# A graph network's layer on one core: projections of x on four 64x64 tiles of the array, with half of x brought across the partitions by DMA, and the second layer's weights prepared earlier

## The chip, the cores and the metric

The kernel runs on one core of a Trainium2 chip. Its time is the device time of one execution in microseconds (us), the median of several executions. The profile is of one such execution; its span, from the first to the last instruction, is somewhat shorter than the time.

## The reference

There are 16 batches of 1024 nodes with 64 channels, and one adjacency matrix of 1024 x 1024. Layer 0 is attention whose weights are multiplied by the adjacency matrix; layer 1 is a diffusion convolution. Each adds its input and normalises. Cut to what matters:

```python
# layer 0: x is (16, 1024, 64), adj (1024, 1024)
Q = einsum('bnc,oc->bno', x, Wq) + bq
K = einsum('bnc,oc->bno', x, Wk) + bk
V = einsum('bnc,oc->bno', x, Wv)
score = softmax(einsum('bnc,bmc->bnm', Q, K), axis=1)   # over the queries n
score = einsum('bnm,mc->bnc', score, adj)
x = layernorm(x + einsum('bnm,bmc->bnc', score, V))
# layer 1: x0 = x, x1 = adj x0, x2 = 2 adj x1 - x0, for two supports that are both adj
x_cat = concatenate([x0, x1, x2, x1, x2], axis=-1)
out = layernorm(x + einsum('bnf,fo->bno', x_cat, weight) + bias)
```

## The kernel before

All is fp32. The batches are worked on in eight pairs (p), so that two times 64 channels fill the 128 partitions. The kernel does three things one after another:

- It forms U = adj x for all batches, a product of 1024 x 1024 x 1024, by seven products of half the size instead of eight (numbered 1 to 7; 2, 3 and 4 are each split again into seven parts). TensorE multiplies, VectorE forms the sums of blocks and adds the results. The left and right sums need room, and they borrow GY, which is not needed yet.
- It runs the attention, pair by pair, in eight steps of 128 nodes (m). The scores are x M x with M = Wq Wk, so that one projection GY = M x + a bias per pair does for both Q and K. A step forms scores on TensorE, VectorE copies them out negated with their least value (e), ScalarE takes the exponentials, TensorE multiplies them with U scaled (us) and sums over the steps (acc). Scores and exponentials run two steps ahead of the multiplication.
- It multiplies adj twice more for layer 1 and normalises.

The projection uses a matrix of 128 x 128 with M in two diagonal blocks and zeros elsewhere (m_w). The code below holds the parts that the change and the prediction touch; xT of a pair is made by eight transposes on TensorE and a copy on ScalarE, and `centre` subtracts the mean of x on GpSimd.

```python
# xT[:, p]: pair p of batches, channels on the partitions (2 x 64), nodes along the row
# GY[:, p]: the projected x of pair p, in the same layout
    def transposed(p, pt=None):

        pt = ps_tile("pt") if pt is None else pt
        for k in range(K8):
            nc.tensor.transpose(pt[:, ts(k, P)], xs[:, p, k, :], ident)
        nc.scalar.activation(xT[:, p], pt, AF.Copy)
    # ...
    def score_weight(pw):
        nc.tensor.transpose(pw[:, 0:P], wq, ident)
        nc.tensor.transpose(pw[:, P : 2 * P], wk, ident)
        nc.vector.tensor_copy(wn, pw[:, 0 : 2 * P].rearrange("p (a o) -> p a o", a=2))

    def score_weight_2(pm):
        nc.tensor.matmul(pm[:, 0:P], wn[:, 1], wn[:, 0], start=True, stop=True)
        nc.tensor.matmul(pm[:, H : H + 1], wn[:, 0], bkp, start=True, stop=True)
        nc.vector.tensor_copy(m_w, pm[:, 0:P])
        nc.vector.tensor_copy(gb, pm[:, H : H + 1])
    # ...
    def project(p, pg=None):
        pg = ps_tile("pg") if pg is None else pg
        for h in range(2):
            nc.tensor.matmul(pg[:, ts(h, H)], m_w, xT[:, p, ts(h, H)], start=True, stop=True)
        nc.scalar.activation(GY[:, p], pg, AF.Identity, bias=gb, scale=1.0)
    # ...
    def layer_weights():
        w24 = const.tile([P, C], FP, tag="w24", name="w24")
        nc.vector.tensor_add(w24, w1s[:, 2], w1s[:, 4])
        nc.vector.tensor_sub(raw[:, 0], w1s[:, 0], w24)
        nc.vector.tensor_add(raw[:, 0], raw[:, 0], ident[:, 0:C])
        nc.vector.tensor_add(raw[:, 0], raw[:, 0], ident[:, C:P])
        nc.vector.tensor_add(raw[:, 1], w1s[:, 1], w1s[:, 3])
        nc.vector.tensor_scalar(raw[:, 2], w24, 2.0, None, op0=ALU.mult)
        rsum = const.tile([P, 5], FP, tag="rsum", name="rsum")
        nc.vector.tensor_reduce(rsum, raw, AX.X, ALU.add)
        nc.vector.scalar_tensor_tensor(
            raw, rsum[:, :, None].to_broadcast([P, 5, C]), -1.0 / C, raw, op0=ALU.mult, op1=ALU.add
        )
        wv = pair_weight("wv")
        for j in range(2):
            s = slice(j * C, (j + 1) * C)
            nc.vector.tensor_copy(wv[s, s], raw[s, 3])
        return wv
    # ... each product of left and right sums is four matmuls deep; step() is its matmuls, some
    # queued VectorE pieces (fill) and the eviction (read); part() is one of seven sub-products
        def step(self, name, g, fills=0, rows=(0, 1)):
            self.matmuls(name, g, rows)
            fill(fills)
            self.read(name, g, rows)
    # ...
    def scores(n):

        p, m = steps[n]
        sc = [ps_tile(f"sc{j}") for j in range(2)]
        for h in range(2):
            for j in range(2):
                s = slice(j * C, (j + 1) * C)
                nc.tensor.matmul(
                    sc[j][:, ts(h, H)], GY[s, p, ts(m, P)], xT[s, p, ts(h, H)],
                    start=True, stop=True,
                )
        NM[n] = small.tile([P, 2], FP, tag="nm", name="nm")
        E[n] = att.tile([P, 2, N], FP, tag="e", name="e", bufs=3)
        for j in range(2):
            nc.vector.tensor_scalar(
                E[n][:, j], sc[j], -1.0, None, op0=ALU.mult, op1=ALU.min,
                accum_out=NM[n][:, j : j + 1],
            )
        SM[n] = small.tile([P, 2], FP, tag="es", name="es")
    # ...
    def weighted(n):
        p, m = steps[n]
        if m == 0:
            ACC[p] = pacc.tile([P, N], FP, tag="acc", name="acc")
        es, us = E.pop(n), US.pop(n)
        for h in range(2):
            for j in range(2):
                nc.tensor.matmul(
                    ACC[p][j * C : (j + 1) * C, ts(h, H)], us[:, j], es[:, j, ts(h, H)],
                    start=(m == 0), stop=(m == K8 - 1),
                )
    # ...
    def centre(p):
        nc.gpsimd.tensor_tensor(
            rows_of(p), rows_of(p), mu[:, p, :, None].to_broadcast([P, G, C]), ALU.subtract
        )
```

The order of work from product 2 to the first steps of the attention (h[0] to h[3] are PSUM tiles; later() queues VectorE pieces, fill and need issue them):

```python
    for q in PARTS:                       # (1, 2, 6, 5, 7, 3, 4)
        first.part(2, q, two, {1: 0, 3: 2, 4: 2}.get(q, 1))
    need("T1", "S1")
    first.step(5, 0, 8)
    # ... product 5's other half, product 3
    score_weight(h[3])
    transposed(0, h[2])
    need("T2")
    lefts, rights = first.halves(4, room[1])
    later("half", lefts)
    later("mu", [
        lambda p=p: nc.vector.tensor_reduce(mu[:, p], rows_of(p), AX.X, ALU.add)
        for p in range(NP)
    ])
    first.step(6, 0, 5)
    score_weight_2(h[3])
    transposed(1, h[2])
    first.step(6, 1, 6)
    project(0, h[3])
    transposed(2, h[2])
    need("S3", "T3")
    line[:0] = [("T4", f) for f in first.right_sum(4)]
    first.step(7, 0, 6)
    project(1, h[3])
    transposed(3, h[2])
    line[:0] = [("half", f) for f in rights]
    first.step(7, 1, 6)
    project(2, h[2])
    project(3, h[3])
    need("T4", "half")
    for q in PARTS:
        first.part(4, q, two)
        if q == 6:
            scores(0)
            for j in range(2):
                exponentials(0, j)
    need("mu")
    nc.vector.tensor_scalar(mu, mu, 1.0 / C, None, op0=ALU.mult)
    nc.sync.dma_start(aT[:, low, right], a_in[:, low, right])
    scores(1)
    for j in range(2):
        exponentials(1, j)
    transposed(4)
    scaled(0)
    wv = layer_weights()
    for p in range(5):
        centre(p)
```

The loop over the steps:

```python
    for n, (p, m) in enumerate(steps):
        if (p, m) == (NP - 2, 2):
            later("half", both(*hop_1.halves(2, room[0])))
        if n + 2 <= last:
            scores(n + 2)
            exponentials(n + 2, 0)
        if p and m > 4:
            weigh(p - 1, m - 5)
        elif p > 1 and m == 0:
            weigh(p - 2, 3)
        elif p == 0 and m:
            if m % 2:
                project(m // 2 + 4)
            else:
                transposed(m // 2 + 4)
                centre(m // 2 + 4)
        if n + 1 <= last:
            scaled(n + 1)
        if m <= 4:
            fill(1)
        weighted(n)
        if m == K8 - 1:
            take(p)
        if n + 2 <= last:
            exponentials(n + 2, 1)
        if p:
            if m == 0:
                norm_1(p - 1)
            elif m == 1:
                norm_2(p - 1)
            elif m == 4:
                transposed(p - 1)
```

Of the kernel before, what the change touches and what calls it, by code (L numbers as in the profile page):

```python
# [9 lines left out]
FP = mybir.dt.float32  # L10
# [8 lines left out]
def gnn_kernel(  # L19
# [13 lines left out]
    nc = tc.nc  # L33
    ctx.enter_context(tc.manual_schedule())
    N, B, C = out.shape
    P = 128
# [3 lines left out]
    H = 512  # L40
# [4 lines left out]
    const = ctx.enter_context(tc.tile_pool(name="const", bufs=1))  # L45
# [5 lines left out]
    def ps_tile(name):  # L51
        return ps.tile([P, 2 * H], FP, tag="ps", name=name)
# [7 lines left out]
    def pair_weight(name):  # L60
        w = const.tile([P, P], FP, tag=name, name=name)
        nc.vector.memset(w, 0.0)
        return w
# [37 lines left out]
    xT = big.tile([P, NP, N], FP, tag="xT", name="xT")  # L101
    GY = big.tile([P, NP, N], FP, tag="gy", name="GY")
    mu = const.tile([P, NP, G], FP, tag="mu", name="mu")
    wn = const.tile([P, 2, P], FP, tag="wn", name="wn")
    m_w = const.tile([P, P], FP, tag="m_w", name="m_w")
    gb = const.tile([P, 1], FP, tag="gb", name="gb")

    def transposed(p, pt=None):

        pt = ps_tile("pt") if pt is None else pt  # L110
        for k in range(K8):
            nc.tensor.transpose(pt[:, ts(k, P)], xs[:, p, k, :], ident)  # L112
        nc.scalar.activation(xT[:, p], pt, AF.Copy)

    def score_weight(pw):
        nc.tensor.transpose(pw[:, 0:P], wq, ident)
        nc.tensor.transpose(pw[:, P : 2 * P], wk, ident)
        nc.vector.tensor_copy(wn, pw[:, 0 : 2 * P].rearrange("p (a o) -> p a o", a=2))

    def score_weight_2(pm):  # L120
        nc.tensor.matmul(pm[:, 0:P], wn[:, 1], wn[:, 0], start=True, stop=True)
        nc.tensor.matmul(pm[:, H : H + 1], wn[:, 0], bkp, start=True, stop=True)
        nc.vector.tensor_copy(m_w, pm[:, 0:P])
        nc.vector.tensor_copy(gb, pm[:, H : H + 1])

    def rows_of(p):
        return xs[:, p].rearrange("p k (b c) -> p (k b) c", b=2)

    def project(p, pg=None):
        pg = ps_tile("pg") if pg is None else pg  # L130
        for h in range(2):
            nc.tensor.matmul(pg[:, ts(h, H)], m_w, xT[:, p, ts(h, H)], start=True, stop=True)  # L132
        nc.scalar.activation(GY[:, p], pg, AF.Identity, bias=gb, scale=1.0)

    def idle_turns(n):
# [12 lines left out]
# [18 lines that stand above are left out]
# [52 lines left out]
    def by_pair(t):  # L218

        return t.rearrange("p k (q f) -> p q k f", f=P)  # L220
# [4 lines left out]
    def later(name, pieces):  # L225
        line.extend((name, piece) for piece in pieces)

    def fill(n):
        for _ in range(min(n, len(line))):
            line.pop(0)[1]()  # L230

    def need(*names):
        while any(name in names for name, _ in line):
            fill(1)
# [159 lines left out]
# [20 lines that stand above are left out]
    def exponentials(n, j):  # L414
        nc.scalar.activation(  # L415
            E[n][:, j], E[n][:, j], AF.Exp, bias=NM[n][:, j : j + 1], scale=-1.0,
            accum_out=SM[n][:, j : j + 1],
        )

    def scaled(n):  # L420

        p, m = steps[n]
        ri = small.tile([P, 2], FP, tag="ri", name="ri")
        nc.vector.reciprocal(ri, SM.pop(n))
        US[n] = small.tile([P, 2, C], FP, tag="us", name="us")
        nc.vector.tensor_tensor(  # L426
            US[n], U[:, m, ts(p, P)].rearrange("p (b c) -> p b c", b=2),
            ri[:, :, None].to_broadcast([P, 2, C]), ALU.mult,
# [13 lines that stand above are left out]
# [7 lines left out]
# [4 lines that stand above are left out]
# [44 lines left out]
    def both(lefts, rights):  # L497
        return [f for pieces in zip(lefts, rights) for f in pieces]

    S = left_tiles()  # L500
    h = [ps_tile("h0"), ps_tile("h1"), pacc.tile([P, N], FP, tag="acc", name="h2"), ps_tile("h3")]
    two = h[2:]
    first = Product(S, xs, by_pair(U), h, None, (2, 3, 4))
# [7 lines left out]
    for n in (1, 2, 4):  # L511
        later(f"S{n}", left_sum(S, n))
    for q in PARTS:
        first.part(2, q, two, {1: 0, 3: 2, 4: 2}.get(q, 1))
    need("T1", "S1")
    first.step(5, 0, 8)
    need("S4")
# [6 lines left out]
    for q in PARTS:  # L524
        first.part(3, q, two)
    score_weight(h[3])
    transposed(0, h[2])
    need("T2")
    lefts, rights = first.halves(4, room[1])
    later("half", lefts)  # L530
# [2 lines left out]
        for p in range(NP)  # L533
    ])
    first.step(6, 0, 5)
    score_weight_2(h[3])
    transposed(1, h[2])
    first.step(6, 1, 6)
    project(0, h[3])
    transposed(2, h[2])  # L540
    need("S3", "T3")
    line[:0] = [("T4", f) for f in first.right_sum(4)]
    first.step(7, 0, 6)
    project(1, h[3])
    transposed(3, h[2])
    line[:0] = [("half", f) for f in rights]
    first.step(7, 1, 6)
    project(2, h[2])
    project(3, h[3])
    need("T4", "half")  # L550
# [10 lines left out]
    for j in range(2):  # L561
        exponentials(1, j)
    transposed(4)
    scaled(0)
    wv = layer_weights()
    for p in range(5):
        centre(p)

# [7 lines left out]
# [8 lines that stand above are left out]
        elif p > 1 and m == 0:  # L584
            weigh(p - 2, 3)
        elif p == 0 and m:
            if m % 2:
                project(m // 2 + 4)
            else:
                transposed(m // 2 + 4)  # L590
                centre(m // 2 + 4)
        if n + 1 <= last:
            scaled(n + 1)
        if m <= 4:
# [13 lines that stand above are left out]
    p = NP - 1  # L608
# [6 lines left out]
    h = [pacc.tile([P, N], FP, tag="acc", name="h0")] + [ps_tile(f"h{n}") for n in (1, 2, 3)]  # L615
# [8 lines left out]
    two = (h[2], h[3])  # L624
# [18 lines left out]
    two = (h[1], h[3])  # L643
# [136 lines left out]
```

## Time and profile before

| what | value |
|---|---|
| time, median of 3 | 621.12 us (620.71 to 621.95) |
| span of the profiled execution | 619.2 us |
| mean granted TensorE clock | 0.986 |
| U = adj x and what is done beside it | to about 113 us |
| attention | about 104 to 417 us |
| layer 1 | from about 417 us on |

The profile's groups that the change touches (line, engine, output<-input, instructions, busy us, mean ns of one): an fp32 matmul shows as two instructions, so the projections of eight pairs are 32 of them.

| group | instructions | mean or median |
|---|---|---|
| L132 PE, projections beside the products (h) | 16 | 592 ns |
| L132 PE, projections in the attention (pg) | 16 | 592 ns, the longest 1220 |
| L133 ACT, their eviction to GY (pg) | 4 | 1094 ns |
| L401 PE, scores, two 64x128 tiles of the array | 512 | 621 ns |
| L438 PE, acc, two 128x64 tiles of the array | 512 | 605 ns |
| L408 DVE, copy of the scores with their least value | 128 | 1222 ns |
| L415 ACT, exponentials | 128 | 1143 ns |

In the profile PE is TensorE's matmuls, PEld its weight loads, DVE VectorE, ACT ScalarE, POOL GpSimd. A busy row gives the time in which an engine had an instruction at work. Matmuls overlap in the pipeline, so their lengths do not add up; the chain of waits gives each piece's share of the path instead. A matmul that stands on two tiles of the array at once shows as two rows of about the same start. An arrow in brackets behind a row of the timeline names the engine and line that ended the idle time before it.

### The profile page before, as it was taken

The numbers are of one execution on the slowest core, as the hardware profiler recorded it, in microseconds if no ns is written. First come the engines' busy times: TensorE is split into PE (matmuls) and PEld (weight loads), VectorE is DVE, ScalarE is ACT, GpSimd is POOL, SyncE is SP. The second block draws the span as 40 slices with busy tenths as digits, with TensorE's granted clock in tenths as the row PEclk, the third lists the DMA queues.
The fourth block names the chain that finished last, engine by engine and source line by source line (L and its number), as shares of the span: only waits on it lengthen the run. The fifth ranks groups of instructions, "written<-read, shape, count | busy, mean of one in ns | idle before, by whom it ended". The sixth has DMA issues, their size and how long they took to land.

```text
span 619.2 us, 6448 instructions
## 1 busy us (share of the span) xinstructions
PE 599.2 (97%) x2478; PEld 305.0 (49%) x2478; DVE 412.8 (67%) x737; ACT 232.8 (38%) x384; POOL 85.8 (14%) x45
## 2 busy tenths in 40 slices
PE   9999999889999999999999999999999999999993
PEld 5747446423334434343443434446647466746463
DVE  0876565755586766778676787855768577648484
ACT  0111032236766667666667766662100000000111
POOL 0000000602130020303002030300000000203366
PEclk9999999969999999999999999999999999999997
DMA  8800002000000000000000000000000000000012
GB/s 264 292 7 1 0 0 69 0 0 2 1 1 1 0 1 2 1 1 0 1 2 0 2 0 1 1 1 1 1 0 0 1 0 1 1 34 35 34 68 103
DMA packets 12575, 14.34 MB, mean 23 GB/s; under 512 B 2304, under 2 KB 7424, under 8 KB 12544
## 3 DMA queue, kind: packets, MB, share of 16 engines
q1 hardware_dynamic: 12544, 13.93, 6.7%
q8 instruction: 19, 0.31, 0.2%
q14 instruction: 12, 0.10, 0.1%
HBM read 9.73 MB, written 4.19 MB: 22 GB/s over the span
## 4 chain that ended last, share of the span: by engine, by line
PE 86%; DVE 6%; DMA 4%; ACT 2%; SPq 1%; issue 1%; DVEq 0%; ACTq 0%
PE h L312 24%; PE sc L401 20%; PE acc L438 19%; PE h L375 13%; DMA xs<-in_x_dram 3%; PE pw L479 3%; PE po L458 2%; PE pt L112 2%; PE pg L132 2%; PE h L132 1%; DVE U L299 1%; DMA aT<-in_adjT_dram 1%; DVE GY L299 1%; DVE e L408 1%; PE h L112 1%; PE h L479 1%
## 5 line engine op out<-in xcount | busy, mean ns | idle before, releaser
L408 DVE TENSOR_SCALAR_CACHE_REDUCE e<-sc 128x1024 f32<-128x1024 f32 x128 | 151.7, 1222 | 64.5 <-PE sc L401 64.5
L415 ACT ACTIVATE e<-e,nm 128x1024 f32<-128x1024 f32 x128 | 146.2, 1143 | 94.7 <-DVE e L408 94.5
L401 PE MATMUL sc<-xT,GY 64*128 64x512 f32 x512 | 131.6, 621 | 4.9 <-DVE e L408 4.9
L438 PE MATMUL acc<-e,us 128*64 128x512 f32 x512 | 124.1, 605 | 0.3 <-DVE us L426 0.3
L175 POOL TENSOR_TENSOR rstd<-var,expo 128x16 f32<-128x16 f32 (+1 forms) x15 | 42.1, 2807 | 381.0 <-DVE var L170 381.0
L312 PE MATMUL h<-T,S 128*128 128x512 f32 x192 | 83.6, 593 | 0.9 <-DVE U L299 0.9
L401 PEld LDWEIGHTS sc<-xT,GY 64*128 64x128 f32 x512 | 45.7, 187 | 78.2 <-issue 46.5
L299 DVE TENSOR_TENSOR U<-h,U 128x512 f32<-128x512 f32 (+1 forms) x58 | 48.2, 837 | 53.1 <-PE h L312 30.2
L438 PEld LDWEIGHTS acc<-e,us 128*64 128x64 f32 x512 | 31.1, 136 | 70.0 <-issue 58.0
L703 ACT ACTIVATE sq<-GY 128x1024 f32<-128x1024 f32 x6 | 6.3, 1057 | 147.9 <-DVE GY L299 147.9
L312 PEld LDWEIGHTS h<-T,S 128*128 128x128 f32 x192 | 36.2, 190 | 44.5 <-issue 42.8
L312 PE MATMUL h<-S,aT 128*128 128x512 f32 x96 | 41.9, 592 | 0.0
L450 POOL TENSOR_TENSOR xs<-xs,mu 128x1024 f32<-128x1024 f32 x8 | 15.1, 1906 | 145.9 <-DVE mu L558 112.7
L375 PE MATMUL h<-xs 128*128 128x256 f32 x144 | 32.6, 382 | 1.4 <-DVE GY L299 1.1
L299 DVE TENSOR_TENSOR GY<-h,GY 128x512 f32<-128x512 f32 (+1 forms) x24 | 19.1, 798 | 16.7 <-PE h L312 11.2
L375 PEld LDWEIGHTS h<-xs 128*128 128x128 f32 x144 | 27.0, 190 | 6.2 <-DVE GY L299 1.5
L312 PEld LDWEIGHTS h<-S,aT 128*128 128x128 f32 x96 | 18.1, 190 | 22.0 <-issue 22.0
L301 ACT ACTIVATE U<-h 128x1024 f32<-128x1024 f32 x8 | 8.0, 1022 | 54.2 <-PE h L312 24.5
L479 PEld LDWEIGHTS pw<-raw,xT 64*128 64x128 f32 x224 | 19.2, 187 | 15.8 <-issue 5.8
L490 DVE TENSOR_TENSOR xT<-pw,raw 128x256 f32<-128x256 f32 x28 | 11.9, 425 | 18.6 <-ACT GY L489 18.6
L415 ACT ACTIVATION_READ_ACCUMULATOR e<-e,nm 128x1 f32 x128 | 24.0, 188 | 0.0
L479 PE MATMUL pw<-raw,xT 64*128 64x192 f32 x224 | 24.0, 332 | 0.0
(165 smaller groups left out, 625.4 us busy)
## 6 DMA issues: line engine op xcount, KB each, us to landing
xs<-in_x_dram SPq DMA_DIRECT2D x16, 256.0 KB, 5.8
aT<-in_adjT_dram SPq DMA_DIRECT2D x16, 256.0 KB, 5.5
out_dram<-GY SPq DMA_DIRECT2D x12, 256.0 KB, 2.2
aT<-in_adjT_dram SPq DMA_DIRECT2D x1, 1024.0 KB, 5.1
out_dram<-GY SPq DMA_DIRECT2D x8, 128.0 KB, 2.0
w1s<-in_w_dram SPq DMA_DIRECT2D x2, 80.0 KB, 2.7
wq<-in_wqT_dram SPq DMA_DIRECT2D x2, 16.0 KB, 4.7
wk<-in_wkT_dram SPq DMA_DIRECT2D x2, 16.0 KB, 3.8
```

The source lines that it names most:

```text
L112: nc.tensor.transpose(pt[:, ts(k, P)], xs[:, p, k, :], ident)
L132: nc.tensor.matmul(pg[:, ts(h, H)], m_w, xT[:, p, ts(h, H)], start=True, stop=True)
L175: nc.gpsimd.tensor_tensor(rstd, var, expo[:, 0:g], ALU.pow)
L299: nc.vector.tensor_add(at(self.res), got, at(self.res))
L312: nc.tensor.matmul(pt[:, ts(i, H)], a[:, k, ts(2 * g + i, P)], b[:, :, k], start=(start and k == 0), stop=(k == HB - 1), skip_group_check= ...
L375: nc.tensor.matmul(pt[:, ts(i, W)], a[:, k, ts(i, P)], b[:, :, k], start=(start and i == k == 0), stop=(k == 1), skip_group_check=True,)
L401: nc.tensor.matmul(sc[j][:, ts(h, H)], GY[s, p, ts(m, P)], xT[s, p, ts(h, H)], start=True, stop=True,)
L408: nc.vector.tensor_scalar(E[n][:, j], sc[j], -1.0, None, op0=ALU.mult, op1=ALU.min, accum_out=NM[n][:, j : j + 1],)
L415: nc.scalar.activation(E[n][:, j], E[n][:, j], AF.Exp, bias=NM[n][:, j : j + 1], scale=-1.0, accum_out=SM[n][:, j : j + 1],)
L438: nc.tensor.matmul(ACC[p][j * C : (j + 1) * C, ts(h, H)], us[:, j], es[:, j, ts(h, H)], start=(m == 0), stop=(m == K8 - 1),)
L450: nc.gpsimd.tensor_tensor(rows_of(p), rows_of(p), mu[:, p, :, None].to_broadcast([P, G, C]), ALU.subtract)
L479: nc.tensor.matmul(pw[:, j, ts(k, 3 * C)], xT[s, p, ts(2 * c + k, P)], raw[s, 0:3].rearrange("p w c -> p (w c)"), start=True, stop=True,)
```

## The change

Four things change. First, a projection no longer multiplies by zeros: M is kept once as 64 columns (m2), and each pair's projection is four matmuls with 64 rows and 64 columns, one on each quarter of the array. [...] A pair has four blocks to project: two batches, each with two halves of its 1024 nodes. Batch 0 lies on the partitions 0 to 63 and batch 1 on 64 to 127, and each result must come out on the same half, which two of the four quarters of the array can do with the data where it is. For the other two the input must lie on the opposite half. So `crossed` brings half of each batch of xT to the other partitions, by two DMA transfers of 64 partitions x 512, into GY of that pair, which is free until the projection's result is written there. Second, the order of transposes and projections around products 6 and 7, and in the steps of pair 0, is shifted so that each transfer has time to land. Third, the preparation of the second layer's weights moves from the start of the attention to behind product 7. Fourth, product 2 has its queued VectorE pieces dealt out differently over its parts.

```diff
--- before.py
+++ after.py
@@ -102,7 +102,7 @@
     GY = big.tile([P, NP, N], FP, tag="gy", name="GY")
     mu = const.tile([P, NP, G], FP, tag="mu", name="mu")
     wn = const.tile([P, 2, P], FP, tag="wn", name="wn")
-    m_w = const.tile([P, P], FP, tag="m_w", name="m_w")
+    m2 = const.tile([P, C], FP, tag="m2", name="m2")
     gb = const.tile([P, 1], FP, tag="gb", name="gb")
 
     def transposed(p, pt=None):
@@ -112,6 +112,12 @@
             nc.tensor.transpose(pt[:, ts(k, P)], xs[:, p, k, :], ident)
         nc.scalar.activation(xT[:, p], pt, AF.Copy)
 
+    def crossed(p):
+
+        for j in range(2):
+            to, of = slice(j * C, (j + 1) * C), slice((1 - j) * C, (2 - j) * C)
+            nc.sync.dma_start(GY[to, p, 0:H], xT[of, p, ts(j, H)])
+
     def score_weight(pw):
         nc.tensor.transpose(pw[:, 0:P], wq, ident)
         nc.tensor.transpose(pw[:, P : 2 * P], wk, ident)
@@ -120,7 +126,9 @@
     def score_weight_2(pm):
         nc.tensor.matmul(pm[:, 0:P], wn[:, 1], wn[:, 0], start=True, stop=True)
         nc.tensor.matmul(pm[:, H : H + 1], wn[:, 0], bkp, start=True, stop=True)
-        nc.vector.tensor_copy(m_w, pm[:, 0:P])
+        for h in range(2):
+            s = slice(h * C, (h + 1) * C)
+            nc.vector.tensor_copy(m2[s], pm[s, s])
         nc.vector.tensor_copy(gb, pm[:, H : H + 1])
 
     def rows_of(p):
@@ -128,8 +136,14 @@
 
     def project(p, pg=None):
         pg = ps_tile("pg") if pg is None else pg
-        for h in range(2):
-            nc.tensor.matmul(pg[:, ts(h, H)], m_w, xT[:, p, ts(h, H)], start=True, stop=True)
+        for turn in range(2):
+            for h in range(2):
+                j = h if turn == 0 else 1 - h
+                rows, cols = slice(h * C, (h + 1) * C), slice(j * C, (j + 1) * C)
+                moving = xT[rows, p, ts(h, H)] if turn == 0 else GY[rows, p, 0:H]
+                nc.tensor.matmul(
+                    pg[cols, ts(h, H)], m2[rows], moving, start=True, stop=True
+                )
         nc.scalar.activation(GY[:, p], pg, AF.Identity, bias=gb, scale=1.0)
 
     def idle_turns(n):
@@ -511,7 +525,7 @@
     for n in (1, 2, 4):
         later(f"S{n}", left_sum(S, n))
     for q in PARTS:
-        first.part(2, q, two, {1: 0, 3: 2, 4: 2}.get(q, 1))
+        first.part(2, q, two, {1: 0, 5: 2, 7: 2}.get(q, 1))
     need("T1", "S1")
     first.step(5, 0, 8)
     need("S4")
@@ -524,7 +538,6 @@
     for q in PARTS:
         first.part(3, q, two)
     score_weight(h[3])
-    transposed(0, h[2])
     need("T2")
     lefts, rights = first.halves(4, room[1])
     later("half", lefts)
@@ -533,18 +546,24 @@
         for p in range(NP)
     ])
     first.step(6, 0, 5)
+    transposed(0, h[2])
+    crossed(0)
     score_weight_2(h[3])
+    first.step(6, 1, 6)
     transposed(1, h[2])
-    first.step(6, 1, 6)
+    crossed(1)
     project(0, h[3])
-    transposed(2, h[2])
     need("S3", "T3")
     line[:0] = [("T4", f) for f in first.right_sum(4)]
     first.step(7, 0, 6)
+    transposed(2, h[2])
+    crossed(2)
     project(1, h[3])
     transposed(3, h[2])
+    crossed(3)
     line[:0] = [("half", f) for f in rights]
     first.step(7, 1, 6)
+    wv = layer_weights()
     project(2, h[2])
     project(3, h[3])
     need("T4", "half")
@@ -561,8 +580,8 @@
     for j in range(2):
         exponentials(1, j)
     transposed(4)
+    crossed(4)
     scaled(0)
-    wv = layer_weights()
     for p in range(5):
         centre(p)
 
@@ -584,11 +603,12 @@
         elif p > 1 and m == 0:
             weigh(p - 2, 3)
         elif p == 0 and m:
-            if m % 2:
-                project(m // 2 + 4)
+            if m in (1, 3, 5):
+                transposed(m // 2 + 5)
+                crossed(m // 2 + 5)
+                centre(m // 2 + 5)
             else:
-                transposed(m // 2 + 4)
-                centre(m // 2 + 4)
+                project((m + 1) // 2 + 3)
         if n + 1 <= last:
             scaled(n + 1)
         if m <= 4:
```

## The prediction

> **What bounds the kernel now.** I read the page's busy table first, then its row of granted clock, then the chain of waits by time, then the busy time by stage (windows that I cut where the chain changes work), and last the timeline of the one stage that stands out. The busy table and the clock row of the page:
>
> ```profile
> PE 599.2 (97%) x2478; PEld 305.0 (49%) x2478; DVE 412.8 (67%) x737; ACT 232.8 (38%) x384; POOL 85.8 (14%) x45
> PEclk9999999969999999999999999999999999999997
> ```
>
> TensorE sets the time nearly everywhere, so a gain has to be TensorE time or one of its few gaps. One slice of the clock row, the ninth (about 124 to 139 us), has lost a third of the clock. Busy time by stage (window, its length, then each engine's busy us and instruction count, clock, DMA):
>
> ```profile
> 59.34:98.56 39.22, 38.66 (x119) 18.93 (x117) 24.48 (x32) 9.04 (x9) 0.00 (x0) 1.00 0.05 17
> 98.56:114.94 16.38, 16.38 (x74) 11.92 (x74) 8.31 (x14) 3.50 (x5) 0.96 (x1) 1.00 0.07 26
> 114.94:136.32 21.38, 16.44 (x46) 5.46 (x46) 15.97 (x29) 8.83 (x13) 8.43 (x5) 0.76 0.00 0
> 136.32:167.84 31.52, 31.52 (x134) 11.64 (x134) 17.50 (x36) 19.16 (x30) 5.71 (x3) 1.00 0.00 1
> 167.84:415.00 247.16, 246.91 (x1258) 102.17 (x1260) 181.29 (x381) 166.38 (x292) 33.80 (x14) 1.00 0.00 1
> ```
>
> The stage 114.94 to 136.32 is the only one here in which TensorE is not busy throughout (16.44 of 21.38 us) and runs at 0.76 of its clock. The timeline (start, length, engine, line, ...) says why:
>
> ```profile
> 113.98 9.38 POOL L450 TENSOR_TENSOR xs<-xs,mu 128x1024 f32<-128x1024 f32 x5 [112.67 <-DVE mu L558]
> ...
> 117.81 1.92 DVE L150 TENSOR_TENSOR w<-w1s 128x64 f32<-128x64 f32 x1
> ...
> 119.77 1.82 DVE L151 TENSOR_TENSOR raw<-w1s,w 128x64 f32<-128x64 f32 x1
> ...
> 121.69 1.75 DVE L152 TENSOR_TENSOR raw<-raw,ident 128x64 f32<-128x64 f32 x1
> 123.48 0.23 DVE L153 TENSOR_TENSOR raw<-raw,ident 128x64 f32<-128x64 f32 x1
> ...
> 126.89 3.78 PE L401 MATMUL sc<-xT,GY 64*128 64x512 f32 x6 [4.63 <-DVE e L408]
> ```
>
> The preparation of the second layer's weights (L150 to L164) keeps VectorE from 117.81 to 125.56, 7.75 us. The scores of step 3 have their first matmul done at 121.6 but find no free PSUM tile until VectorE has read those of step 2, after 125.60: a gap of 4.63 us, and after it six half-matmuls take 3.78 us and the projection behind them 3.71 us instead of 1.91. Three of the eleven preparation instructions take 1.75 to 1.92 us where L153, of the same shape, takes 0.23: they stand beside five GpSimd centrings of 9.38 / 5 = 1.88 us each.
>
> The projections, from the same timeline (each fp32 matmul shows as two instructions, its halves):
>
> ```profile
> 94.97 3.60 PE L132 MATMUL h<-xT,m_w 128*128 128x512 f32 x8
> ...
> 97.35 2.37 ACT L133 ACTIVATE GY<-h,gb 128x1024 f32<-128x1024 f32 x2
> ...
> 98.51 3.72 PE L375 MATMUL h<-T,aT 128*128 128x256 f32 x16
> ...
> 142.97 1.98 PE L132 MATMUL pg<-xT,m_w 128*128 128x512 f32 x4
> ```
>
> The two full-array matmuls of one pair show as x4 and put 1.91 us on the chain of waits in the attention, 1.72 among the full-array matmuls of products 6 and 7. The four matmuls of acc, on two 128x64 tiles, show as x8 and cost only 1.87 on the chain: two tiles run at the same time. The front ends in a row of waits: projection 2 is done long before 98.51, but product 4 needs its PSUM tile, and ScalarE has copied that only at 98.46.
>
> [...] the scores' half-matmuls start in pairs 6 to 7 ns apart, 0.43 us from pair to pair, and 0.1 us is lost at the first. No run here shows four. [...]
>
> **The change part by part.**
>
> 1. *Weights behind product 7.* The eleven VectorE instructions move to behind the eviction of the last block of product 7, when GpSimd has no work (0.00 busy in 59.34 to 98.56). By their own rows [...] they cost 5 x 0.23 + 0.19 + 0.49 + 0.49 + 0.17 + 0.39 = 2.9 us. Product 7's eviction ends at 96.4 by the old clock; VectorE is then busy until 99.3, one sum of x (1.21) later 100.5, and its next eviction was wanted at 100.61. That just fits, and the sub-product that needs the evicted bank starts another 1.7 us later. I put 0 for it on the path.
> At the old place the chain had, from 114.94: scores 1's two evictions, scores 2 (end 119.27), acc 0, scores 3, projection 4, acc 1, end 136.32. Without the 7.75 us, scores 3 follows acc 0 at once: 119.27 + 1.87 + 1.92 = 123.06 instead of 130.66, so 7.6 us gone. The projection there (3.71, half clock) gives way to a transpose block (1.02, as at 138.23 on the chain): 2.7 gone. acc 1 stays (1.87 against 1.94). Sum 10.35 us.
>
> 2. *Projections in the attention.* Before, steps 2 to 7 of pair 0 carry three transposes (1.02) and three projections (1.91): 8.79 us. After, by the order of instructions, they carry two transposes and four projections. On four tiles a projection is two turns of 0.43 us, with the 0.1 us of a mode change[...]: I take 1.0. So 2.04 + 4.0 = 6.04, and 2.75 us gone. All of it is on the path: the stage 136.32 to 167.84 has TensorE busy 31.52 of 31.52 us, ScalarE 19.16 and VectorE 17.50.
>
> 3. *The front, 59.34 to 98.56.* Gone: the wait of 0.7 us before the first transpose (product 6 comes first now and its tile is free), and 0.7 at projection 0 (1.72 to 1.0). But the two transposes of pairs 2 and 3 now use one PSUM tile with only projection 1 between. The second waits until ScalarE has copied the first, ScalarE first copies the block of product 7 (1.02), and that copy waits for VectorE's addition (1.23): 1.25 + 1.0 + 1.0 = 3.3 us after product 7, while TensorE has only 0.87 + 1.0 us of work. A new wait of 1.4 us, which eats what projection 1 gives (0.7) and more. Behind the second half of product 7, TensorE must wait for ScalarE's copy of projection 2 as before (chain: 95.13 to 98.51 = 3.38 us, whatever the projections take), so projections 2 and 3 give nothing. By adding up: products 6 and 7 at 59.5, 67.6, 76.3 and 87.4 (start), product 4 at 97.6 instead of 98.51: 0.9 us gone.
>
> 4. *Moves of halves by DMA.* Sixteen transfers of 128 KB. The row of stores of 128 KB in the page has 2.0 us from issue to landing. Each is issued one stage (at least 6.9 us, or two steps of 4.8) before the projection that needs it. 0 on the path.
>
> 5. *Small moves.* m2 takes two copies for one (some 0.1 us of VectorE, hidden). The new split of fills in product 2 lets the last addition before product 5 start as its matmul ends instead of 0.15 us later: 0.15 gone.
>
> Sum: 10.35 + 2.75 + 0.9 + 0.15 = 14.15 us. What follows 167.84 is the same instruction for instruction, and TensorE-bound (246.91 of 247.16), so it only shifts. 621.12 - 14.15 = 607.0; I add 0.2 for small waits between the shorter projections: 607.2.
>
> **The rivals.**
> *Four tiles run only two at a time.* For: no run shows four[...]. Against: on the timeline at 116.21 one score tile's two weight loads stand alone, because the other waited for its buffer, and at 117.36 four follow together; so the next matmul of the free tile ran beside the delayed one, and each tile takes its own work; and the two matmuls on one half of the rows write different partitions of a bank, as acc does. Then a projection costs 1.9 as before: 4 x 0.9 + 0.7 is lost, 611.5.
> *The gap changes place.* For: the new wait of 1.4 us before transpose 3, and VectorE is full behind product 7; if the eleven instructions took 4.5 us, product 4 would be late by 0.6 or so. [...] Against: the gaps I can count are 1.4 us.
> *A transfer lands late.* For: all sixteen go through one queue, behind a 1 MB reload (5.1 us). Against: the reload is issued after the first eight, and the next is 20 us later. If it happens, 1 to 2 us: 609.
> *ScalarE or VectorE becomes the bound in pair 0.* ScalarE needs 2 x 1.15 + 1.1 = 3.4 us a step, VectorE 3.2, TensorE still 4.8. No change.
>
> **Range and chances.** The 10.35 us of part 1 is the firmest term; the 2.75 depends on four tiles and the 0.9 on the waits. With both halved and a further 0.5 us lost somewhere the result is 609.6; with a projection at 0.9 and no wait at transpose 3, 605.2. Range 605.0 to 610.6. 2% is 608.7: within the range, on the slow side, and 1.5 us from my figure. Faster by over 2%: 0.75; within: 0.24; slower: 0.01.
>
> **What the changed profile would show.** Right: the ninth slice of the clock row at 9; the eleven instructions with no row over 0.5 us, between product 7 and the next eviction; projection groups of x8 at about 1.0 us on the chain, with half-matmuls starting in fours; a wait of TensorE for ScalarE of 1 to 1.5 us before the last transpose of the front; pair 0's last step ending about 14 us earlier. Wrong: projections of 1.9 us or starts in pairs; a granted clock of 0.5 anywhere between 60 and 170; TensorE waiting for a DMA; or the shift of 14 us shrinking after pair 0.

## The result, and the profile after

The changed kernel takes 607.4 us (606.94 to 607.56, four executions) against 620.99 (620.71 to 621.95, four executions of the kernel before). The ratio is 0.9777, with a 95% interval of 0.976 to 0.9794: 13.6 us, or 2.2%, faster. The prediction was 607.2. The span of the profiled execution is 605.6 us.

The page's busy row and clock row of the kernel after:

```profile
PE 588.4 (97%) x2510; PEld 299.8 (49%) x2510; DVE 408.5 (67%) x738; ACT 232.7 (38%) x384; POOL 85.8 (14%) x45
PEclk9999999999999999999999999999999999999997
```

The ninth slice has its clock back. TensorE is busy 10.8 us less, VectorE 4.3 us less. Busy time by stage, in windows cut at the same work as before (the columns are the same):

```profile
59.67:98.53 38.86, 35.97 (x135) 16.78 (x133) 25.56 (x40) 9.22 (x10) 0.00 (x0) 1.00 0.17 43
98.53:114.97 16.44, 16.44 (x73) 11.98 (x74) 10.22 (x19) 3.34 (x5) 0.97 (x1) 1.00 0.07 27
114.97:126.03 11.06, 10.74 (x50) 4.28 (x50) 8.81 (x18) 7.21 (x12) 10.25 (x6) 1.00 0.10 24
126.03:154.87 28.84, 28.84 (x147) 9.59 (x146) 17.43 (x37) 19.96 (x31) 3.92 (x3) 1.00 0.12 28
154.87:401.93 247.06, 246.81 (x1258) 102.02 (x1260) 181.29 (x381) 167.00 (x292) 33.80 (x14) 1.00 0.00 1
```

Read against the stages of before: the third row took 21.38 us and takes 11.06, at full clock. The fourth took 31.52 and takes 28.84, and TensorE is still busy throughout. The last, 247.05 us from 167.84 to 414.89 before, has only moved. The first row is the surprise: TensorE has 2.7 us less to do there, but the stage is hardly shorter (38.86, and 39.22 before), so its work has become waiting.

The timeline after, at the places that answer to those shown of before:

```profile
86.12 1.02 ACT L113 ACTIVATE xT<-h 128x1024 f32<-128x1024 f32 x1
...
87.19 1.09 PE L112 MATMUL h<-ident,xs 128*128 128x128 f32 x8 [1.40 <-ACT xT L113]
...
96.91 0.23 DVE L166 TENSOR_TENSOR raw<-raw,ident 128x64 f32<-128x64 f32 x1
...
98.53 3.72 PE L389 MATMUL h<-T,aT 128*128 128x256 f32 x16 [1.50 <-ACT GY L147]
...
127.88 0.65 PE L144 MATMUL pg<-xT,m 64*64 64x512 f32 x2
127.90 0.65 PE L144 MATMUL pg<-GY,m 64*64 64x512 f32 x2
128.36 0.59 PE L144 MATMUL pg<-xT,m 64*64 64x512 f32 x2
128.38 0.60 PE L144 MATMUL pg<-GY,m 64*64 64x512 f32 x2
128.90 1.51 PE L452 MATMUL acc<-e,us 128*64 128x512 f32 x6
```

Of the last five rows four are one projection and the fifth is the work behind it. Two matmuls with xT and two with the moved half start within some 20 ns, and their second halves follow 0.48 us later, before the first, 0.65 us long, have ended; the next work starts 1.02 us after the first. That is four tiles at once. The preparation row that took 1.75 us takes 0.23. And TensorE waits twice for ScalarE in the front, 1.40 and 1.50 us.

The start of every later piece depends on when the input lands, which moves by about 1 us from run to run: the second part of product 3 begins at 48.70 us in the profile of before, at 49.04 after, and between 48.26 and 49.30 in the experiments. Stages are therefore compared by their lengths below: *front* is from that part to product 4, *head* is from product 4 to pair 0's output projection (po).

| | front | head | time, us |
|---|---|---|---|
| before | 48.70 to 98.56: 49.86 | 98.56 to 171.62: 73.06 | 620.99 |
| after | 49.04 to 98.53: 49.49 | 98.53 to 158.66: 60.13 | 607.40 |

From po on both kernels keep the same distance, 12.96 us, to the last normalisation (613.85 and 600.89); the rest of the difference of the spans, 0.64 us, is in the last stores.

### The profile page after: what moved, and what is told of

Its sections match the earlier page's. It is cut to its first block, busy times and chain, and to the rows that moved or that the text cites. A ratio compares the mean times of both kernels' runs of the same rounds, so it can differ in the third digit from the quotient of the medians.

```text
span 605.6 us, 6563 instructions
## 1 busy us (share of the span) xinstructions
PE 588.4 (97%) x2510; PEld 299.8 (49%) x2510; DVE 408.5 (67%) x738; ACT 232.7 (38%) x384; POOL 85.8 (14%) x45
## 4 chain that ended last, share of the span: by engine, by line
PE 88%; DVE 5%; ACT 2%; DMA 2%; SPq 1%; issue 1%; DVEq 0%; ACTq 0%
PE h L326 25%; PE sc L415 21%; PE acc L452 19%; PE h L389 15%; PE pw L493 3%; PE po L472 2%; DMA xs<-in_x_dram 2%; PE pt L112 2%; DVE U L313 1%; DVE GY L313 1%; SPq L77 1%; PE pg L144 1%; PE h L493 1%; PE h L112 0%; DVE var L196 0%
## 5 line engine op out<-in xcount | busy, mean ns | idle before, releaser
L415 PE MATMUL sc<-xT,GY 64*128 64x512 f32 x512 | 128.7, 615 | 0.3 <-DVE e L422 0.3
```

The costliest lines, as they stand in the source:

```text
L415: nc.tensor.matmul(sc[j][:, ts(h, H)], GY[s, p, ts(m, P)], xT[s, p, ts(h, H)], start=True, stop=True,)
```

## The experiments

Each kernel was timed beside the kernel before, whose median in these groups was 620.8 to 621.6 us. A time "above after" is taken from the changed kernel's 607.40 us, measured in another group, so the lengths of the stages are the firmer comparison.

**The weights alone.** The kernel before, with one line moved:

```diff
     first.step(7, 1, 6)
+    wv = layer_weights()
     ...
     scaled(0)
-    wv = layer_weights()
```

> The kernel before with one thing changed: the second layer's weights are prepared behind product 7. Theory (the long stay of VectorE starves the scores, and the gap then halves the clock): the scores of step 3 follow acc at once, 7.6 us, and the projection of pair 4 runs at full clock, 3.71 to 1.91, so 9.4 us gone: 611.6. The clock row shows no dip. Rival (VectorE behind product 7 is full, and the next eviction comes late): 1 us or more given back there, 612.6 or above. Rival (the change's gain comes from the projections): about 619.

Measured: 611.49 us (611.28 to 611.67), ratio 0.9845 (0.983 to 0.986). Head 98.25 to 161.90 = 63.65, 9.41 us less than before; front 49.87, as before. Timeline of this kernel behind product 7:

```profile
95.99 0.22 DVE L150 TENSOR_TENSOR w<-w1s 128x64 f32<-128x64 f32 x1
...
98.93 1.22 DVE L532 TENSOR_REDUCE mu<-xs 128x16 f32<-128x1024 f32 x1
100.29 0.69 DVE L299 TENSOR_TENSOR U<-h,U 128x512 f32<-128x512 f32 x1
```

The eleven instructions take from 95.99 to 98.91, 2.9 us. Product 4's first eviction starts at 100.29, 2.10 us after its first matmul (98.19), just as in the kernel before (98.51 and 100.61): nothing is given back. The first theory's number is met.

**The weights put back** into the changed kernel.

```diff
     first.step(7, 1, 6)
-    wv = layer_weights()
     ...
     scaled(0)
+    wv = layer_weights()
```

> The changed kernel with the weights put back to the start of the attention, all else kept. Theory: the gap of more than 4 us and the half clock return, 9.4 us as in the reverse step, so about 616.8. Rival (with shorter projections TensorE has less to do there, so the delay hides less, or the half clock falls on other work): 618 or more. Rival (the weights were worth little): under 611.

Measured: 616.25 us (615.75 to 616.96). Head 97.95 to 168.07 = 70.12, which is 9.99 us longer than after. Timeline of this kernel, then its clock in three windows:

```profile
121.14 1.75 DVE L166 TENSOR_TENSOR raw<-raw,ident 128x64 f32<-128x64 f32 x1
...
126.33 3.78 PE L415 MATMUL sc<-xT,GY 64*128 64x512 f32 x6 [4.62 <-DVE e L422]
```

```profile
120.00:124.00 4.00, 1.70 (x6) 0.29 (x2) 3.79 (x7) 0.00 (x0) 2.81 (x2) 1.00 0.29 66
...
130.00:134.00 4.00, 4.00 (x15) 2.34 (x16) 1.60 (x4) 2.98 (x4) 1.90 (x1) 0.50 0.00 0
...
136.00:138.00 2.00, 2.00 (x16) 0.51 (x12) 0.60 (x1) 0.00 (x0) 0.00 (x0) 1.00 0.03 8
```

The gap is back (4.62 us) and so is the half clock, 0.50 while TensorE is fully busy. The kernel before has, behind its gap of 4.63 us,

```profile
127.00:135.00 8.00, 8.00 (x14) 2.63 (x16) 4.27 (x10) 4.08 (x7) 0.00 (x0) 0.53 0.00 0
```

which is 0.53 over eight us of a busy TensorE. In the profiles the weights are worth 9.41 us in one direction and 9.99 in the other; by the medians it is 9.34 (620.83 to 611.49) and 8.85 (607.40 to 616.25). So most of it comes with either kind of projection. In the profiles the clock makes the difference: it returns 7.6 us after TensorE starts again in the kernel before and 8.8 us after it here (by windows in the last section), and half of the 1.2 us between is lost.

**The centrings held back.** The kernel before, with the weights at their old place, but GpSimd starting its centrings after them:

```diff
-    nc.vector.tensor_scalar(mu, mu, 1.0 / C, None, op0=ALU.mult)
     ...
     wv = layer_weights()
+    nc.vector.tensor_scalar(mu, mu, 1.0 / C, None, op0=ALU.mult)
     for p in range(5):
         centre(p)
```

> The kernel before with the weights at their old place; only the scaling of the means, which starts GpSimd's five centrings, comes after the weights instead of before. Theory (three of the eleven instructions waited for GpSimd [...]): they take 2.9 us instead of 7.75, the scores of step 3 wait under 1 us, the clock stays, about 8.5 us gone: 612.5. Rival (it is the place and the number of instructions, whatever GpSimd does): 619 to 621. Rival (the conflict moves to the us multiplications of the next steps, up to 1.9 us each): 614 to 616.

Measured: 612.39 us (612.12 to 612.85), ratio 0.9858 (0.9842 to 0.9874). Timeline of this kernel:

```profile
117.99 0.22 DVE L150 TENSOR_TENSOR w<-w1s 128x64 f32<-128x64 f32 x1
118.24 0.23 DVE L151 TENSOR_TENSOR raw<-w1s,w 128x64 f32<-128x64 f32 x1
118.57 0.23 DVE L152 TENSOR_TENSOR raw<-raw,ident 128x64 f32<-128x64 f32 x1
...
121.29 7.53 POOL L450 TENSOR_TENSOR xs<-xs,mu 128x1024 f32<-128x1024 f32 x4 [119.99 <-DVE mu L565]
...
123.55 1.65 DVE L426 TENSOR_TENSOR us<-U,ri 128x128 f32<-128x128 f32 x1
```

The three instructions take 0.22 to 0.23 us as soon as GpSimd is not at work, the eleven 2.9 us. The collision has moved to us, which takes 1.65 us where it takes 0.29 undisturbed; TensorE does not need us then, so it costs nothing. What is left is the 2.9 us that VectorE still stays at the old place: on the chain the scores of step 3 take 2.76 us instead of 1.92, and the head, 98.93 to 163.42 = 64.49 us, is 0.84 longer than with the weights moved. Most of what the move of the weights brings could be had without moving them: 8.4 of 9.3 us, both against 620.83. It was the meeting of two engines, not the place, that made the gap long: three preparation instructions in the kernel before (1.75 to 1.92 us against 0.23) and us here (1.65 against 0.29), all with two inputs, took most of the length of a centring of 1.9 us. What the two engines contend for is not shown by the runs.

**The projections on the full array**, in the changed kernel's order; the transfers are left out, since nothing reads them.

```diff
-        for turn in range(2):
-            for h in range(2):
-                ... four matmuls m2[rows] x moving, 64 rows to 64 columns
+        for h in range(2):
+            nc.tensor.matmul(pg[:, ts(h, H)], m_w, xT[:, p, ts(h, H)], start=True, stop=True)
```

> The changed kernel with its order of work, but with projections on the full array with the zero blocks, and no transfers. Theory (four tiles run at once, 1.02 us on the chain against 1.91): four projections in the attention at 0.9 each and 0.7 of projection 0 are lost, projections 1 to 3 lie beside waits for ScalarE: 4.3 us, 611.7. Rival (the order of work gives the gain, not the tiles): 607.4 to 608. Rival (projections 1 to 3 are on the path too): 614.

Measured: 612.24 us (612.18 to 612.42), 4.84 above after. Head 99.21 to 162.85 = 63.64, 3.51 us longer than after; front 50.05 (from 49.16), 0.56 longer; the rest is the landing of the input (0.12) and the last stores (0.6). Chain of waits of this kernel, front and attention (start, length, what):

```profile
75.94 1.72 PE h L136 x4
77.66 6.88 PE h L316 x16
...
87.81 1.09 PE h L112 x8
...
95.78 3.43 PE h L136 x8
...
128.57 1.91 PE pg L136 x4
```

In the attention a projection costs 1.91 and not 1.02: 4 x 0.89 = 3.56, against the 3.51 found. This head is as long as that of the weights alone (63.65), so in the attention the new order adds nothing by itself, and the two parts, 9.41 and 3.51, make up the whole 12.93. In the front projections 2 and 3 (3.43) fill the time in which TensorE of the changed kernel waits for ScalarE, so on four tiles they gain next to nothing there. It also shows that the changed order by itself is no gain: this front, 50.05, is longer than the front before, 49.86, although the first wait is gone.

**The old order of steps** in the attention, each projection one step behind its transposes:

```diff
-            if m in (1, 3, 5):
-                transposed(m // 2 + 5); crossed(m // 2 + 5); centre(m // 2 + 5)
-            else:
-                project((m + 1) // 2 + 3)
+            if m % 2:
+                project(m // 2 + 4)
+            else:
+                transposed(m // 2 + 4); crossed(m // 2 + 4); centre(m // 2 + 4)
```

> The changed kernel with transposes and projections of pairs 4 to 7 in the old order, each projection one step behind its transposes. Theory (a transfer lands 6.4 us after the transposes start, by the profile: 2.6 until ScalarE has copied, 0.6 more to issue, 2.3 to land; the projection would come after 4.8): three waits of 1.6 us, 4.8 lost, 612.2. Rival (the transfer is quick enough): 607.4.

Measured: 612.25 us (611.63 to 613.09), 4.85 above after. Timeline of this kernel, one projection:

```profile
127.10 1.09 PE L112 MATMUL pt<-ident,xs 128*128 128x128 f32 x8
...
129.67 1.00 ACT L113 ACTIVATE xT<-pt 128x1024 f32<-128x1024 f32 x1
...
130.70 1.10 SPq L119 DMA_DIRECT2D GY<-xT  x2
131.91 1.07 PE L144 MATMUL pg<-xT,m 64*64 64x512 f32 x4
132.91 0.19 PEld L144 LDWEIGHTS pg<-GY,m 64*64 64x64 f32 x2 [0.82 <-DMA GY<-xT]
132.92 1.73 PE L144 MATMUL pg<-GY,m 64*64 64x512 f32 x4
```

Transposes at 127.10, copied at 130.67, sent, and the weight loads of the matmuls with the moved half wait for the DMA, so that these matmuls end 1.65 us late. The projection takes 2.65 to 2.72 us on the chain, three times; the head, 97.75 to 162.86 = 65.11 us, is 4.98 longer than after. So the new order is needed for the transfers: without it four tiles would lose more here (5.0) than they bring in the attention (3.5).

**Each transfer made twice**, the second after the first:

```diff
-        for j in range(2):
+        for j in (0, 1, 0, 1):
             nc.sync.dma_start(GY[to, p, 0:H], xT[of, p, ts(j, H)])
```

> The changed kernel with each pair's two transfers made twice, one after the other, so that a pair's data lands about 3 us later. Theory (every transfer has 3.5 us or more to spare, but for pair 3 just before product 4): 607.4, up to 608 if pair 3 is late. Rival (transfers are near the path or disturb the engines): 609 or more.

Measured: 607.29 us (606.72 to 607.59); projections stay at 1.02 us on the chain. In the trace the issuing of transfers, from the first to the last, takes 25.32 us in the front and 29.71 in the attention, against 21.75 and 27.47 after: the last ones go out 3.6 and 2.2 us later, and all land 2.2 us (median) to 4.0 us (longest) after their issue. The transfers have that much to spare with the new order, and their doubled traffic disturbs nothing.

**One transpose earlier.** The changed kernel, with pair 2's transposes ahead of product 7:

```diff
     project(0, h[3])
+    transposed(2, h[2])
+    crossed(2)
     ...
     first.step(7, 0, 6)
-    transposed(2, h[2])
-    crossed(2)
     project(1, h[3])
```

> The changed kernel with one thing moved: pair 2's transposes and transfer come ahead of product 7's first half, not behind it, so that pair 3's transposes no longer wait for ScalarE (1.40 us idle in the profile). Theory: product 7's second half starts 1.2 to 1.4 us earlier, and everything behind it: 606.1. Rival (TensorE would then only wait longer for ScalarE before product 4): 607.4.

Measured: 605.84 us (605.36 to 605.98), ratio to before 0.9744 (0.9731 to 0.9757). Chain of waits:

```profile
84.54 1.02 PE h L144 x8
85.55 1.02 PE h L112 x8
86.58 6.88 PE h L326 x16
```

Projection 1, the transposes of pair 3 and product 7 follow each other without a gap. Front 48.14 us, 1.35 less than after. The wait for ScalarE, 1.40 us, was worth nearly what the profile says of it.

**Both waits.** In addition, product 7's second block is copied after the projections, and the weights are prepared before it:

```diff
-    first.step(7, 1, 6)
+    first.matmuls(7, 1)
+    fill(6)
     wv = layer_weights()
     project(2, h[2])
     project(3, h[3])
+    first.read(7, 1)
```

> The same, and in addition the projections of pairs 2 and 3 come ahead of the eviction of product 7's second half, so that ScalarE copies projection 2 first, and the weights are prepared while VectorE waits for product 7 (5.24 us idle). Theory: the second wait of TensorE (1.50 us before product 4) shrinks to 0.3, another 1.2 us: 604.9. Rival (the late copy of product 7's block delays the evictions of product 4): 606 to 606.5.

Measured: 605.05 us (604.63 to 606.84), ratio to before 0.974 (0.9723 to 0.9757). Front 49.30 to 96.37 = 47.07, another 1.07 less. Chain of waits:

```profile
94.06 1.11 PE h L144 x8
95.18 0.02 issue
95.20 1.12 ACT GY L147
96.33 0.04 issue
96.37 5.45 PE h L389 x24
```

ScalarE now copies projection 2 at once, and product 4 waits for that copy alone. The times differ by 0.79 us and the executions of the two kernels overlap; it is the front that shows this step.

**All of ScalarE's copies of product 7 last.** The order of the changed kernel, with both blocks of product 7 copied late:

```diff
-    first.step(7, 0, 6)
+    first.matmuls(7, 0)
+    fill(6)
     transposed(2, h[2])
     crossed(2)
+    first.read(7, 0)
     project(1, h[3])
     ...            # and the second block as in the last experiment
```

> The changed kernel's order, but with ScalarE's copy of each of product 7's two blocks issued after its copies for the next pairs: pair 2's transposes come ahead of the eviction of the first half, projections 2 and 3 and the weights ahead of that of the second. Theory (both waits are ScalarE's order, not its work): product 2's second part to product 4 takes 49.49 us in the changed kernel, 47.07 with the transposes moved ahead and the second copy late; here pair 2's transposes have nothing to wait for, another 0.4 us: 46.7, and 604.6 in all. Rival (the late copy holds up what adds to U): 606 or more.

Measured: 605.08 us (604.44 to 605.79), front 48.44 to 95.56 = 47.12: no better than the last. I had expected pair 3's transposes not to wait; the chain of waits has

```profile
83.30 0.89 PE h L112 x8
84.19 0.02 issue
84.21 1.03 ACT xT L113
85.25 0.04 issue
85.29 1.09 PE h L112 x8
```

Pair 3's transposes still wait for ScalarE's copy out of the one tile, 1.10 us, in which projection 1 (1.02) just fits; I had left this out. In both orders one projection hides beside one copy, and it does not matter which.

**The old fills** of product 2 in the changed kernel:

```diff
-        first.part(2, q, two, {1: 0, 5: 2, 7: 2}.get(q, 1))
+        first.part(2, q, two, {1: 0, 3: 2, 4: 2}.get(q, 1))
```

> The changed kernel with product 2's queued VectorE pieces dealt out as before. Theory (the last addition before product 5 is held up by a piece in front of it): 0.15 us later, 607.5, less than the start of the input moves from run to run; in the trace the last addition of product 2 starts with a gap of 0.15 us after its matmul. Rival (more than one addition waits): 608 or more.

Measured: 606.98 us (606.8 to 607.29), the wrong way by 0.4, which is less than the landing of the input moves. In the trace, from the last part of product 2 to product 5: 29.71 to 32.53 = 2.82 us, and 30.34 to 33.01 = 2.67 after. The timeline of this kernel has the addition behind two others:

```profile
30.59 1.28 DVE L228 TENSOR_TENSOR S<-aT 128x512 f32<-128x512 f32 x2
31.79 0.68 DVE L313 TENSOR_TENSOR U<-h,U 128x512 f32<-128x512 f32 x1
```

The 0.15 us are there in the stage; in the time they cannot be seen.

## Why the prediction was right, step by step

| step | predicted, us | measured, us | from |
|---|---|---|---|
| weights behind product 7 | 7.6 + 1.8 = 9.4 (the 10.35 also swaps a projection for transposes) | 9.41, head | weights alone |
| four tiles in the attention | 4 x 0.9 = 3.6 | 3.51, head | full array against after |
| one projection | 1.0 | 1.02 | chain after |
| whole head | 10.35 + 2.75 = 13.1 | 73.06 - 60.13 = 12.93 | before and after |
| front | 0.9 | 49.86 - 49.49 = 0.37 | before and after |
| new fills | 0.15 | 2.82 - 2.67 = 0.15 | old fills |
| transfers | 0 | 0 | doubled transfers |
| sum | 14.15, less 0.2 for small waits | 13.45 | |

The sum of the stages, 13.45, and the difference of the times, 13.59, agree within what the landing of the input and the last stores move. The steps that carried the prediction held:

- That the long stay of VectorE makes the gap, that the half clock comes with the gap, and that both go with the weights' move. The first is shown from both sides (weights alone, weights back). The clock's half is a link by occurrence: in the attention it is there in both kernels with a gap of 4.6 us, whose profiled executions have a mean granted clock of 0.986 and 0.987; those of all the others have 0.994 to 0.997. In the kernel after, with its waits of 1.40 and 1.50 us, the clock is 1.00 from 59.67 to 114.97. How long a gap has to be is not shown. No experiment makes a gap there without VectorE's delay, but the kernels before and after both end with one: once TensorE has no more work the clock falls to half as well (before 0.50 from 612.5 us to the end, after 0.50 from 599.3, TensorE 0.00 busy).
- That three instructions waited for GpSimd: shown by the centrings held back.
- That four tiles run at once: until then the author's estimate from the pairs of two tiles; shown by the starts of the rows (within some 20 ns) and by the full array (1.91 us on the chain against 1.02).
- That everything behind pair 0 only shifts: 12.96 us all the way from the first to the last anchor.
- That VectorE's load behind product 7 just fits: product 4's first eviction starts 0.15 us after the sum of x before it ends (99.26 + 1.22, then 100.63), and as long after product 4's start as before, 2.10 us.

The step that was off is *the front*, by 0.53 us. Its new wait was sized right: 3.27 us from the end of product 7's half to pair 3's transposes, 3.3 predicted. What I had left out is that three groups of matmuls took 0.1 to 0.2 us longer here: one after a wait, one after a few very short matmuls and one after a change of the array's tiling. The chain of waits after has

```profile
67.97 6.97 PE h L326 x16
...
76.84 7.08 PE h L326 x16
...
87.19 1.09 PE h L112 x8
```

Product 7's first half behind a projection on 64x64 tiles takes 7.08 us and not 6.87; pair 3's transposes after their wait 1.09 and not 0.87; and product 6's second half, behind the very short matmuls that make M, 6.97. That is 0.53 together. The full array, with the same order of work, has the 1.09 and the 6.97 as well but 6.88 for product 7, so 0.2 us goes with the tiles and the rest with the order. I counted 0.1 us for the change of tiling in the projection's own 1.0 and nothing for the change back.

That the time came within 0.2 us of the prediction is partly luck. The stages gave 0.70 us less than predicted: 0.53 in the front and 0.17 in the head. Three things that have nothing to do with the argument made up for most of it: the 0.2 us put in for small waits, which the head's last steps did not need (28.84 of 28.84 us busy); 0.14 from the landing of the input and the last stores; and a median of the kernel before of 620.99 instead of 621.12. One reading in the prediction is off too: the first matmul of the scores of step 3 ends at 122.26, where the gap of 4.63 us begins, and not at 121.6. Nothing in its sum rests on that.

The rivals: two tiles at a time is refuted by the trace. Late transfers are refuted for this order, and would have been right for the old one. ScalarE or VectorE as the bound is refuted by TensorE's 28.84 of 28.84 us. The gap that changes place did so in a small form: not at VectorE but at ScalarE, 1.40 and 1.50 us, with the clock at 1.00. The reordered kernels took most of that back; they are the ones that beat both, at 605.05 us (both waits), though by no more than 2.4 us over the changed kernel.

## What to carry to other kernels

When an instruction takes eight times as long as another of its shape, look for what the other engines did in that time before moving it: here a later start of GpSimd gave 8.4 of the 9.3 us that the move gave. A long stay of VectorE that starved TensorE was charged twice here, once for the gap of 4.6 us and once for the clock after it; waits of 1.5 us, with the clock at 1.00, were charged once. Where TensorE waits for a copy, as in this front, making its work shorter makes only the wait longer; here the order of the copies on ScalarE was the lever, and it is read from what ScalarE did between the matmul's end and the copy that released the tile.

## What the runs showed of the hardware that was not expected

- Where the tiling of the array changed, 0.1 to 0.2 us was lost on each side. In the attention the projection's first halves start 0.52 us after the scores' last (127.36, then 127.88) and acc starts 0.52 us after the projection's last (128.38, then 128.90), against 0.43 us from pair to pair of the scores' halves. The sixteen half-matmuls of product 7 behind a projection took 7.08 us, against 6.88 behind one on the full array.
- The clock stayed low for 7.6 and 8.8 us after TensorE was busy again. In the kernel with the weights put back TensorE has worked without a break since 126.33, and the clock is 0.50 until about 135.1 (0.93 over the window 135 to 136), 8.8 us. In the kernel before TensorE works from 126.89 and the clock is back at about 134.5 (0.75 over 134 to 135), 7.6 us. There it had fallen at about 124.3 (0.82 over 124.2 to 124.3), 2.0 us after TensorE's last matmul ended (122.26).
- A us multiplication, 0.29 us undisturbed, took 1.65 us beside GpSimd's centrings in one kernel and 0.47 to 0.64 in others (0.47 and 0.64 in the kernel before), by where in a centring it fell: after, one from 125.66 to 126.29 (0.63 us) stands beside a centring that ends at 126.15.
